# A transformer block with two mixtures of experts: a fixed order for TensorE in the first stage, counts made last, sixteen zero products, and three shared experts ahead of the tiles

## The chip, the cores and the metric

The kernel runs on one core of one Trainium2 chip. That core has five engines with a queue each: TensorE (PE, matrix products; its weight loads are shown apart as PEld), VectorE (DVE), ScalarE (ACT), GpSimd (POOL) and SyncE (SP, which here only issues DMAs). Sixteen DMA engines move the data. The metric is the time of one execution on the device in microseconds, lower is better. Before the change the median of 9 runs is 551.19 us (546.62 to 552.5).

## What is computed

The input x has 4 blocks of 512 rows with 256 columns. It goes through half a feed-forward layer, an attention and the same half layer again:

```python
x = x + 0.5 * ffn(layernorm(x))
x = x + attn(layernorm(x))     # 3 heads of width 256, mean over the heads, then fc_w, fc_b
x = x + 0.5 * ffn(layernorm(x))

def ffn(x):                    # 16 experts, the best 2 of each row
    scores = sigmoid(x @ gate_w)
    selected = top_k(scores + expert_bias, 2)
    top = scores[selected] / sum(scores[selected])
    shared = (silu(x @ shared_gate_w) * (x @ shared_up_w)) @ shared_down_w
    routed = sum(comb[:, e] * ((silu(g_e) * u_e) @ experts_down[e]) for e in range(16))
    return shared + routed     # g_e, u_e = split(x @ experts_gate_up[e])
```

Everything is float32. The attention's softmax runs over the axis of the queries, and the kernel works with A = Wq^T Wk / 16 and G = Wv^T fc_w^T / 3 for each head, which it makes once in the first stage.

## The kernel before

**Stages.** In the profiled execution the first stage lasts until 80 us: x and all weights are loaded, all four blocks b are normalised and routed, A and G are made, and two shared experts are computed. Then come 42 expert tiles of 128 rows each (80 to 151 us), a branch for more tiles that only an uneven routing needs, the other two shared experts, and the attention, block by block (168 to 434 us). From its second block on, the attention's loop also normalises and routes the block before for the second feed-forward layer. At the end come that layer's tiles and shared experts.

**Order.** The program is written for a scheduler that places each instruction in its engine's queue by priority, which follows the program text, and by an estimate of when its inputs are ready. Engines run their queues strictly in order; across engines there are semaphores. Three helpers bend the order without adding a wait on other engines: `after(ins, other)` (L184) puts one instruction behind another of its engine, `tc.issue_after(ins)` does so for all that a `with` block issues on the engine of `ins`, and `apart` (L189) declares that two accesses don't touch the same rows.

**One block in the first stage.** `moments(b)` (L196) makes mean and variance on DVE, the root on ACT and the reciprocal on DVE. `layernorm_T` (L215) normalises the rows to `xn` (on DVE for block 0, L233; on ACT for blocks 1 to 3, L228), transposes them on TensorE (L238), copies the two halves `xnT` out of PSUM (L242 on ACT, L244 on ACT or L246 on DVE) and doubles `xn` on ACT (L248), because each row is sent to two experts. `scores` (L282) multiplies with `gate_w` (L290, sixteen products of 16 columns a block), and `gate` (L298) takes the sigmoid. `router` (L308) picks the best two on DVE, counts on TensorE, with ten bfloat16 products against a matrix of ones or a triangle (L349 to L359), how many rows of the same expert stand ahead, and gets from that each row's place in a buffer sorted by expert. It also adds the block to the running count `seen`, makes the column totals `counts` with one more product (L374), and has POOL write the 512 rows twice to that buffer in DRAM, in 8 indirect DMAs (L393, "scatters").

**From the router to the tiles.** `ends` (L402) makes the end of each expert's rows from the last `counts`. `blanks` (L409, L417) writes 128 empty rows behind each expert's end, a DMA each on SP, whose place SP reads from `end` (L412). `early` (L465) computes on DVE a table of the first 9 tiles, which only blocks 0 to 2 can fill; `table` (L490) that of the rest. `load` (L503, L511) reads the place of a tile from the table into a register of SP and loads its rows as `xg`; `experts` (L549) runs a tile through transposes (L556), products (L572), sigmoid (L578), a second transpose (L587) and the down product (L594), and has POOL scatter the result (L599). SP's queue holds the first 8 blanks, the 9 first loads, the other 8 blanks, and then the rest.

**Shared expert.** `shared` (L522) makes `pg` and `pu` with four products of 512 columns each (L529) in two PSUM buffers, sigmoid on ACT (L534), two products on DVE (L535, L536), eight products `po` of 256 columns (L541), and adds them to x on DVE (L546). Its `pg` and `pu` share three PSUM buffers ("mm") with A and G (L713, copied out by ACT at L717).

**The first stage's text (L664 to L733).** Block 0: moments, scores; then moments 1, gate 0, router 0, scores 1, gate 1, moments 2 and 3, router 1, then for blocks 2 and 3 scores, gate, router, and last `ends` and `early`. A and G stand behind the ranks of router 0, shared experts 0 and 1 behind A and G and behind the early table, `table` behind those.

Of the kernel before, what the change touches and what calls it, by code (L numbers as in the profile page):

```python
# [17 lines left out]
P = 128  # L18
# [3 lines left out]
def tile_macaron_block(  # L22
# [62 lines left out]
    MAGIC = 12582912.0  # L85
    CEIL = 0.5 - 1.0 / (2 * P)
# [17 lines left out]

    xs = []
    for b in range(B):
        xb = acts.tile([P, NJ, H], F32, tag=f"x{b}", name=f"x{b}")
        nc.sync.dma_start(out=xb, in_=x[b].rearrange("(p j) h -> p j h", j=NJ))
        xs.append(xb)
# [73 lines left out]

    def after(ins, other):  # L184

        info = mybir.DependencyInfo(mybir.DependencyClass.NoSync, mybir.DependencyReason.DATA)
        tc.add_manual_dep(ins.ins, other.ins.name, info, reason="order")
# [6 lines left out]
    turned, rooted = {}, {}  # L194
# [20 lines left out]
    def layernorm_T(b, which, dispatch=False, moms=None):  # L215
# [10 lines left out]
        for j in range(NJ):  # L226
            if off is not None:
# [4 lines left out]
            else:  # L232
                nc.vector.tensor_scalar(  # L233
# [3 lines left out]
            for c in range(NC):  # L237
                nc.tensor.transpose(  # L238
                    pts[c][:, j * P : (j + 1) * P], xn[0][:, j, c * P : (c + 1) * P], ident
                )  # L240
        xnT = acts.tile([P, NC, N], F32, tag=f"xnT{b}", name=f"xnT_{n}")
        ins = nc.scalar.copy(xnT[:, 0, :], pts[0])  # L242
        if off is not None:
            ins = nc.scalar.copy(xnT[:, 1, :], pts[1])  # L244
        else:
            turned[n] = nc.vector.tensor_copy(xnT[:, 1, :], pts[1])  # L246
        if dispatch:
            after(nc.scalar.copy(xn[1][:, :, 0:H], xn[0][:, :, 0:H]), ins)  # L248
        return xnT, xn

    class Ffn:


        def __init__(self, which):
# [25 lines left out]
            self.xn, self.s, self.got = {}, {}, {}  # L280

        def scores(self, b, moms=None):  # L282
# [4 lines left out]
            for j in range(NJ):  # L287
                t = b * NJ + j
                for c in range(NC):
                    self.scored = nc.tensor.matmul(  # L290
# [5 lines left out]
                    )  # L296
# [12 lines left out]
        def router(self, b):  # L309
# [39 lines left out]
            nc.tensor.matmul(rank[:, 0:n], ones, over_t(region), start=True, stop=False)  # L349
            nc.tensor.matmul(rank[:, 0:n], ones, over_t(self.seen[:, b, :]), start=False, stop=False)  # L350
            for k in range(NK):
                for j in range(NJ - 1):
                    nc.tensor.matmul(
                        rank[:, (j + 1) * NE : n], ones,
                        ones_k[:, k, j : j + 1, :].to_broadcast([P, NJ - 1 - j, NE]),
                        start=False, stop=False,
                    )
            for k in range(NK):
                self.ranked = nc.tensor.matmul(  # L359
                    rank[:, 0:n], before, ones_k[:, k], start=False, stop=(k == NK - 1)  # L360
                )
# [12 lines left out]
            nc.tensor.matmul(  # L374
                self.counts[:, b * NE : (b + 1) * NE], ones, self.seen[:, b + 1, :],
                start=True, stop=True,
            )
# [23 lines left out]

        def ends(self):  # L402
# [6 lines left out]
        def blanks(self, e0=0, e1=NE):  # L409

            for e in range(e0, e1):
                r = nc.values_load(  # L412
                    self.end[0:1, e : e + 1], engines=(mybir.EngineType.SP,),
# [3 lines left out]
                ins = nc.sync.dma_start(  # L417
# [105 lines left out]
        def shared(self, b, cols=P):  # L523
# [3 lines left out]
            for ps, wt in ((pg, sg), (pu, su)):  # L527
                for c in range(NC):
                    nc.tensor.matmul(  # L529
                        ps, wt[:, c, :], self.xnT[b][:, c, :], start=(c == 0), stop=(c == NC - 1)  # L530
                    )
            h = work.tile([P, N], F32, tag="h", name=f"h_{n}")
            g = work.tile([P, N], F32, tag="g", name=f"g_{n}")
            nc.scalar.activation(g, pg, AF.Sigmoid)  # L534
            nc.vector.tensor_tensor(g, g, pg, ALU.mult)  # L535
            nc.vector.tensor_tensor(h, g, pu, ALU.mult)  # L536
            for j0 in range(0, NJ, 2):
                po = psum.tile([P, 2, H], F32, tag="dn", name=f"po_{n}_{j0}")
                for j in (j0, j0 + 1):
                    for p0 in range(0, P, cols):  # L540
                        self.shared_on_pe = nc.tensor.matmul(  # L541
                            po[p0 : p0 + cols, j - j0, :],
                            h[:, j * P + p0 : j * P + p0 + cols], sd, start=True, stop=True,
                        )
                xp = xs[b][:, j0 : j0 + 2, :]
                last = nc.vector.scalar_tensor_tensor(xp, po, 0.5, xp, ALU.mult, ALU.add)  # L546
            return last

# [120 lines left out]
    with tc.issue_after(turned["ln0_0"].ins):  # L669
# [3 lines left out]
    with tc.issue_after(m[1][3].ins):  # L673
        ffn.router(0)
    ranked = ffn.ranked
    ffn.scores(1, m[1])
    scored = [ffn.scored]
    ffn.gate(1)
    with tc.issue_after(ffn.last.ins), tc.issue_after(ffn.gated.ins):
        m.extend(moments(b, f"ln0_{b}", True) for b in (2, 3))  # L680
    with tc.issue_after(m[3][3].ins):
        ffn.router(1)
    for b in (2, 3):
        ffn.scores(b, m[b])
        ffn.gate(b)
        with tc.issue_after(ffn.last.ins):
            ffn.router(b)
    with tc.issue_after(ffn.last.ins):
        ffn.ends()
        ffn.early()  # L690


    with tc.issue_after(ranked.ins):
        fcT = weights.tile([P, NC, H], F32, tag="fcT", name="fcT")
        for c in range(NC):
            pt = psum.tile([P, H], F32, tag="dn", name=f"ptfc_{c}")
            for o in range(NC):
                nc.tensor.transpose(
                    pt[:, o * P : (o + 1) * P], fcw[:, o, c * P : (c + 1) * P], ident
                )  # L700
            nc.scalar.copy(fcT[:, c, :], pt)
        A, G = [], []
        for h in range(NH):
            wq, wk, wv = (wi[:, h] for wi in watts)
            for res, name, lhs, rhs, by in (
                (A, "A", wq, wk, float(H) ** -0.5),
                (G, "G", wv, fcT, 1.0 / NH),
            ):
                t = weights.tile([P, NC, H], F32, tag=f"{name}{h}", name=f"{name}{h}")
                pw = psum.tile([P, NC, H], F32, tag="mm", name=f"pw{name}{h}")  # L710
                for ec in range(NC):
                    for c in range(NC):
                        made = nc.tensor.matmul(  # L713
                            pw[:, ec, :], lhs[:, c, ec * P : (ec + 1) * P], rhs[:, c, :],
                            start=(c == 0), stop=(c == NC - 1),
                        )
                nc.scalar.mul(t, pw, by)  # L717
                res.append(t)


    done = ffn.last
    for b in (0, 1):
        with tc.issue_after(made.ins), tc.issue_after(done.ins):
            done = ffn.shared(b)
    with tc.issue_after(done.ins):
        ffn.table()
    ffn.blanks(0, NE // 2)
# [18 lines left out]
    for b in range(B // 2, B):  # L746
        ffn.shared(b)
    for b in range(B):
# [41 lines left out]
        if b > 0:  # L790
# [3 lines left out]
            if b == B - 1:  # L794
                ffn2.early()
# [29 lines left out]
    ffn2.router(B - 1)  # L825
# [78 lines left out]
```

## Time and profile before

| what | before |
|---|---|
| median of 9 runs | 551.19 us |
| the profiled execution | 553.12 us |
| its span | 551.3 us |
| TensorE busy, whole span | 502.8 us (91%) |
| weight loads, DVE, ACT, POOL busy | 355.9, 276.2, 191.5, 161.7 us |
| mean granted TensorE clock | 0.964 |

The span runs from the first to the last instruction of the program, the profiled execution's own time contains 1.8 us more around it. Busy times are sums over an engine's instructions; those of TensorE are modelled at their ends. The next lines are the page's slices: the span in 40 equal parts of 13.8 us, each digit the busy share in tenths, for TensorE, DVE, ACT, POOL and the mean DMA engine. The first six digits are the first stage.

```profile
PE   4789399999989999999999999999999967999984
DVE  4556155545745651158702676144482642455565
ACT  3471015666540620018200382004600323466630
POOL 2456504555530100001050011400032063356550
DMA  7993355557210100110021100100014044546755
```

In lists of the timeline a line gives the start and length in microseconds, the engine (SPq is SP's queue, which only issues), the line of the kernel, the operation, what is written from what, the shapes, how many instructions are merged, and in brackets how long the engine had been idle and what ended that ("issue" or "remote" where the profile names no one).

### The profile page before, as it was taken

The page shows a single profiled execution, that of the slowest core. Times are in us where ns is not written, and L with a number is a line of the kernel's source. Part 1 is how long each engine was busy: PE and PEld are TensorE (multiplying, and loading weights), DVE is VectorE, ACT ScalarE, POOL GpSimd, SP SyncE. Part 2 cuts the span into 40 slices and gives each one's busy share as a digit, 9 for nine tenths or more (in the row PEclk, how much of TensorE's full clock was granted, in tenths as well). Part 3 has the DMA queues.
Part 4 walks back from the last instruction along what each step waited for, and adds up shares of the span by engine and source line. Part 5 has one row for each costly group of instructions (what it writes and reads, how often), then busy time and mean ns, then how long its engine had stood idle before and what let it go on. Part 6 is the DMA issues. An engine that isn't in the chain of part 4 may idle for free. (4 is left out here: it accounts for less than half of the span.)

```text
span 551.3 us, 7562 instructions
## 1 busy us (share of the span) xinstructions
PE 502.8 (91%) x2120; PEld 355.9 (65%) x2120; DVE 276.2 (50%) x985; ACT 191.5 (35%) x446; POOL 161.7 (29%) x195
## 2 busy tenths in 40 slices
PE   4789399999989999999999999999999967999984
PEld 3577058888645478744886458854688644778842
DVE  4556155545745651158702676144482642455565
ACT  3471015666540620018200382004600323466630
POOL 2456504555530100001050011400032063356550
PEclk9998779999989999999999999999999896999989
DMA  7993355557210100110021100100014044546755
GB/s 265 356 366 132 125 147 162 164 165 238 102 46 0 39 0 1 38 38 2 0 78 38 38 2 10 68 0 0 1 38 117 9 145 154 153 146 182 261 182 191
DMA packets 38427, 57.89 MB, mean 105 GB/s; under 512 B 5360, under 2 KB 30192, under 8 KB 38384
## 3 DMA queue, kind: packets, MB, share of 16 engines
q1 hardware_dynamic: 30176, 37.49, 21.9%
q0 software_dynamic: 7104, 19.47, 9.8%
q10 hardware_dynamic: 1104, 0.42, 0.3%
q8 instruction: 19, 0.31, 0.2%
q14 instruction: 24, 0.20, 0.1%
HBM read 31.04 MB, written 26.31 MB: 104 GB/s over the span
## 5 line engine op out<-in xcount | busy, mean ns | idle before, releaser
L393 POOL DMA_INDIRECT xn_d<-xn_ln,pos x64 | 62.5, 976 | 154.5 <-DVE v L807 73.8
L599 POOL DMA_INDIRECT y_d<-ey,to x84 | 82.1, 977 | 72.4 <-ACT xt L560 47.6
L572 PE MATMUL peg<-gu,xt 128*128 x336 | 88.5, 387 | 1.9 <-issue 1.2
L773 PE MATMUL psc<-y,xnT_lna 128*128 128x512 f32 x192 | 84.5, 595 | 0.4 <-ACT ex L780 0.4
L815 PE MATMUL pa<-v,ex 128*128 128x256 f32 x384 | 83.5, 379 | 0.0
L815 PEld LDWEIGHTS pa<-v,ex 128*128 128x128 f32 x384 | 73.0, 190 | 9.9
L773 PEld LDWEIGHTS psc<-y,xnT_lna 128*128 128x128 f32 x192 | 36.0, 190 | 44.4 <-issue 42.2
L572 PEld LDWEIGHTS peg<-gu,xt 128*128 128x128 f32 x336 | 58.3, 193 | 9.4 <-issue 2.9
L780 ACT ACTIVATE ex<-psc,nmax 128x512 f32<-128x512 f32 x48 | 32.8, 686 | 85.4 <-DVE nmax L777 84.2
L589 DVE COPY hT<-pht 128x128 f32<-128x128 f32 x84 | 24.4, 290 | 65.1 <-issue 21.2
L594 PE MATMUL pey<-dn,hT 128*128 x168 | 51.8, 391 | 1.8 <-DVE hT L589 1.8
L598 ACT ACTIVATE ey<-pey,xg 128x256 f32<-128x256 f32 x84 | 39.6, 473 | 28.4 <-issue 16.9
L751 POOL TENSOR_TENSOR x<-x,fcb_bc 128x1024 f32<-128x1024 f32 x4 | 9.4, 2351 | 129.8 <-DVE xn_lna L233 129.8
L777 DVE TENSOR_REDUCE nmax<-psc 128x1 f32<-128x512 f32 x48 | 32.9, 686 | 26.1 <-PE psc L773 26.1
L803 PE MATMUL pv<-G,xnT_lna 128*128 128x256 f32 x192 | 44.6, 385 | 0.0
L758 PE MATMUL py<-xnT_lna,A 128*128 128x512 f32 x96 | 42.0, 592 | 0.0
L820 DVE TENSOR_TENSOR x<-x,pa 128x256 f32<-128x256 f32 x16 | 6.7, 421 | 68.9 <-PE pa L815 68.9
L803 PEld LDWEIGHTS pv<-G,xnT_lna 128*128 128x128 f32 x192 | 35.1, 190 | 4.3
L578 ACT ACTIVATE sig<-peg 128x128 f32<-128x128 f32 x84 | 23.3, 278 | 41.4 <-PE peg L572 20.2
L560 ACT COPY xt<-pxt 128x256 f32<-128x256 f32 x84 | 30.6, 366 | 12.0 <-PE pxt L556 10.2
L556 PE MATMUL pxt<-ident,xg 128*128 128x128 f32 x168 | 33.1, 281 | 0.0
L758 PEld LDWEIGHTS py<-xnT_lna,A 128*128 128x128 f32 x96 | 18.2, 190 | 21.3 <-issue 21.0
(164 smaller groups left out, 630.2 us busy)
## 6 DMA issues: line engine op xcount, KB each, us to landing
xg<-xn_d SPq DMA_DIRECT2D x84, 129.0 KB
xn_d<-nowhere SPq DMA_DIRECT2D x34, 129.0 KB
gu<-ffn_experts_gate_up_dram SPq DMA_DIRECT2D x4, 1024.0 KB
yg<-y_d SPq DMA_DIRECT2D x8, 512.0 KB
y<-y_d SPq DMA_DIRECT2D x6, 512.0 KB
x<-in_L_attn_x_dram SPq DMA_DIRECT2D x4, 512.0 KB
dn<-_L_ffn_experts_down_dram SPq DMA_DIRECT2D x2, 1024.0 KB
out_dram<-x SPq DMA_DIRECT2D x3, 512.0 KB
```

The costliest lines, as they stand in the source:

```text
L393: ins = nc.gpsimd.indirect_dma_start(out=self.xn_v[k * NT + b * NJ + j], out_offset=bass.IndirectOffsetOnAxis(ap=pos[:, k, j : j + 1], axi ...
L556: ins = nc.tensor.transpose(pt[:, c, :], xg[:, c * P : (c + 1) * P], ident)
L572: nc.tensor.matmul(pg, xt[:, c, :], gu[:, bass.ds(e, 1), c, :], start=(c == 0), stop=(c == NC - 1),)
L594: self.downed = nc.tensor.matmul(py, hT, dn[:, bass.ds(e, 1), :], start=True, stop=True)
L598: nc.scalar.mul(y, py, xg[:, H + 1 : W])
L599: ins = nc.gpsimd.indirect_dma_start(out=self.y_v[i], out_offset=bass.IndirectOffsetOnAxis(ap=tos[i], axis=0), in_=y, in_offset=None,)
L758: nc.tensor.matmul(py, A[h][:, c, fc * P : (fc + 1) * P], xnT[:, c, :], start=(c == 0), stop=(c == NC - 1),)
L773: nc.tensor.matmul(pscore, xnT[:, c, m * P : (m + 1) * P], ys[h][:, c, :], start=(c == 0), stop=(c == NC - 1),)
L777: nc.vector.tensor_reduce(nmax[:, m : m + 1], pscore, AX.X, ALU.max, negate=True)
L780: nc.scalar.activation(ex[:, m, :], pscore, AF.Exp, bias=nmax[:, m : m + 1], accum_out=z[:, m : m + 1],)
L803: nc.tensor.matmul(pv, xnT[:, c, m * P : (m + 1) * P], G[h][:, c, :], start=(c == 0), stop=(c == NC - 1),)
L815: nc.tensor.matmul(pa, es[h][:, m, j * P : (j + 1) * P], vs[h][:, m, :], start=(h == 0 and m == 0), stop=(h == NH - 1 and m == NJ - 1),)
```

## The change

- **Loads.** x of block 0 is loaded in two halves of two row groups each.
- **Zero products.** At the very start DVE clears a tile of 128 x 512 bfloat16, and TensorE multiplies it sixteen times (`WARM = 16`) into a PSUM buffer that nobody reads.
- **A fixed order on TensorE.** Each group of TensorE's instructions in the first stage gets a name (`mark`), and `in_turn` puts every instruction of a group behind the last of the group before, over 39 named groups: T is a transpose of a block, S its scores, K and L the ranks for the first and second choice, A, fcT and G the attention's weights, U and D the two halves of a shared expert, C the counts.
- **The text's order.** Router 1 now comes directly behind router 0, and the moments of blocks 2 and 3 behind router 1. A and G come ahead of scores 2 and 3. The up half of shared expert 0 stands between scores 3 and router 2, its DVE products between router 2 and router 3. Counts of all four blocks come behind router 3 (in the second layer, three of them ahead of its early table and the last behind its last router). Behind `ends` come shared expert 1, the early table, shared expert 2, the second table.
- **Shared experts.** Three instead of two ahead of the tiles, so only number 3 is left between the tiles and the attention.
- **Smaller moves.** Block 1 is normalised on DVE instead of ACT, the second half of block 0's transposed rows is copied by ACT instead of DVE, the doubling copies of blocks 0 and 1 and the copy of block 1's transposed rows stand behind a sigmoid on ACT. The ranks of the first choice are all issued ahead of those of the second. `blanks` gets parameters for another queue, which no call uses.

```diff
+    idle = const.tile([P, 512], BF16, tag="idle", name="idle")
+    nc.vector.memset(idle, 0.0)
+    nothing = psum.tile([P, 512], F32, tag="mm", name="nothing")
+    for _ in range(WARM):
+        nc.tensor.matmul(nothing, idle[:, 0:P], idle, start=True, stop=True)
...
+        for j in range(0, NJ, 2 if b == 0 else NJ):
+            js = slice(j, j + (2 if b == 0 else NJ))
+            nc.sync.dma_start(out=xb[:, js], in_=rows[:, js])
...
+    def mark(name, ins):
+        groups.setdefault(name, []).append(ins)
+        return ins
+    def in_turn(*names):
+        for one, two in zip(names, names[1:]):
+            for ins in groups[two]:
+                after(ins, groups[one][-1])
...
-            if off is not None:
+            if off is not None and n != "ln0_1":
                 nc.scalar.activation(xn[0][:, j, 0:H], ...
...
-        if off is not None:
+        if off is not None or n == "ln0_0":
             ins = nc.scalar.copy(xnT[:, 1, :], pts[1])
...
             for k in range(NK):
                 for j in range(NJ - 1):
-                    nc.tensor.matmul(
-                        rank[:, (j + 1) * NE : n], ones,
+                    count(
+                        "KL"[k], rank[:, (j + 1) * NE : n], ones,
                         ones_k[:, k, j : j + 1, :].to_broadcast([P, NJ - 1 - j, NE]),
-            for k in range(NK):
-                self.ranked = nc.tensor.matmul(
-                    rank[:, 0:n], before, ones_k[:, k], start=False, stop=(k == NK - 1)
-                )
+                count("KL"[k], rank[:, 0:n], before, ones_k[:, k], stop=(k == NK - 1))
...
-            nc.tensor.matmul(
-                self.counts[:, b * NE : (b + 1) * NE], ones, self.seen[:, b + 1, :],
-                start=True, stop=True,
-            )
...
+        def count(self, b0, b1):
+            for b in range(b0, b1):
+                mark(f"C{self.w}_{b}", nc.tensor.matmul(
+                    self.counts[:, b * NE : (b + 1) * NE], ones, self.seen[:, b + 1, :],
+                    start=True, stop=True,
+                ))
```

The first stage's text after the change, with the loops that make A and G left out:

```diff
     ffn.scores(0, m[0])
-    with tc.issue_after(turned["ln0_0"].ins):
+    with tc.issue_after(normed["ln0_0"].ins), tc.issue_after(copied["ln0_0"].ins):
         m.append(moments(1, "ln0_1", True))
     with tc.issue_after(rooted["ln0_1"].ins):
         ffn.gate(0)
+    ffn.scores(1, m[1])
+    after(copied["ln0_1"], ffn.gated)
+    after(doubled["ln0_0"], ffn.gated)
+    with tc.issue_after(normed["ln0_1"].ins):
         ffn.router(0)
     ffn.gate(1)
+    after(doubled["ln0_1"], ffn.gated)
+    with tc.issue_after(ffn.last.ins):
+        ffn.router(1)
     with tc.issue_after(ffn.last.ins), tc.issue_after(ffn.gated.ins):
         m.extend(moments(b, f"ln0_{b}", True) for b in (2, 3))
...
+    for b in (2, 3):
+        ffn.scores(b, m[b])
+        with tc.issue_after(rooted["ln0_3"].ins):
+            ffn.gate(b)
+    ffn.shared_up(0)
+    with tc.issue_after(m[3][3].ins):
+        ffn.router(2)
+    with tc.issue_after(ffn.last.ins):
+        ffn.shared_down(0)
+    with tc.issue_after(ffn.gated_up.ins):
+        ffn.router(3)
+    ffn.count(0, B)
+    with tc.issue_after(ffn.last.ins):
+        ffn.ends()
+    with tc.issue_after(ffn.last.ins):
+        ffn.shared(1)
+    with tc.issue_after(ffn.gated_up.ins):
+        ffn.early()
+    with tc.issue_after(ffn.last.ins):
+        done = ffn.shared(2)
     with tc.issue_after(done.ins):
         ffn.table()
+    in_turn(
+        "Tln0_0", "S0_0", "Tln0_1", "S0_1", "K0_0", "L0_0", "A00", "A01", "A10", "K0_1", "A11",
+        "L0_1", "A20", "A21", "fcT", "G00", "G01", "G10", "G11", "G20", "G21",
+        "Tln0_2", "S0_2", "Tln0_3", "S0_3", "K0_2", "L0_2", "U0_0", "K0_3", "L0_3", "C0_0",
+        "C0_1", "C0_2", "C0_3", "D0_0", "U0_1", "D0_1", "U0_2", "D0_2",
+    )
     ffn.blanks(0, NE // 2)
...
-    for b in range(B // 2, B):
-        ffn.shared(b)
+    ffn.shared(3)
...
             if b == B - 1:
+                ffn2.count(0, B - 1)
                 ffn2.early()
...
     ffn2.router(B - 1)
+    ffn2.count(B - 1, B)
```

## The prediction

> **What bounds the kernel now.** I first read the busy time by stage (stretch and its length, busy us of PE, weight loads, DVE, ACT and POOL, granted clock, DMA share, GB/s).
>
> ```profile
> 0.00:80.00 80.00, 55.00 (x226) 40.47 (x227) 36.95 (x171) 26.18 (x46) 35.13 (x64) 0.89 0.72 235
> 80.00:151.40 71.40, 69.84 (x380) 57.30 (x378) 42.71 (x206) 43.22 (x125) 38.95 (x42) 1.00 0.53 164
> 151.40:168.00 16.60, 14.93 (x46) 8.62 (x47) 7.64 (x14) 6.81 (x10) 4.39 (x4) 0.90 0.12 43
> 168.00:434.00 266.00, 265.06 (x1009) 176.87 (x1007) 128.20 (x347) 69.40 (x136) 31.70 (x35) 1.00 0.08 27
> ```
>
> TensorE idles 25 us in the first 80 and hardly at all from there to 434. A microsecond off the first stage is one off the end, and TensorE work taken from the later stages into those idle 25 us is gained too. Then the timeline of the first stage on POOL (start, length, what, idle before and its releaser): the first scatter of row blocks 0, 1 and 2, and the last of all.
>
> ```profile
> 19.30 1.15 POOL L393 DMA_INDIRECT xn_d<-xn_ln,pos  x1 [15.34 <-DVE st_ln L201]
> 33.20 0.98 POOL L393 DMA_INDIRECT xn_d<-xn_ln,pos  x1 [3.52 <-DVE xn_ln L388]
> 45.38 0.99 POOL L393 DMA_INDIRECT xn_d<-xn_ln,pos  x1 [2.06 <-ACT fcT L701]
> 64.50 0.97 POOL L393 DMA_INDIRECT xn_d<-xn_ln,pos  x1 [0.30 <-issue]
> ```
>
> Neighbours start 1.27 us apart, so 32 scatters need 40.8 us; they took 46.2, with two waits for a router of 3.5 and 2.1 us. Last, the timeline between the blanks' first issue and the first expert tile.
>
> ```profile
> 51.38 8.90 SPq L417 DMA_DIRECT2D xn_d<-nowhere  x4
> 60.33 0.20 DVE L461 TENSOR_REDUCE fe<-fp 128x1 f32<-128x48 f32 x1 [1.27 <-DVE fo L457]
> 61.73 0.60 ACT L717 ACTIVATE A<-pwA 128x512 f32<-128x512 f32 x1 [10.58 <-issue]
> 68.19 0.60 ACT L717 ACTIVATE G<-pwG 128x512 f32<-128x512 f32 x1 [5.86 <-remote]
> 70.06 7.55 SPq L511 DMA_DIRECT2D xg<-xn_d  x9
> 79.86 0.60 PE L556 MATMUL pxt<-ident,xg 128*128 128x128 f32 x4
> ```
>
> From about 52.7 to 68.3, while SP's blanks and POOL's scatters run together, nearly every wait is late: a blank takes 2.2 us (0.83 after 78), a dependent DVE step 1.4 us, and ACT takes up a product that ended at 52.2 only at 61.7. I call this **the slow stretch**. The second layer shows it again, from 446 to 457.6, where blanks and scatters overlap too (DVE waits 9.2 us there). It ends 2.8 us after the last scatter's issue ends (65.47). TensorE then does three quarters of two shared experts in 11.5 us, from 68.3 to the tiles at 79.86, at a granted clock of 0.5 until 74.8.
>
> **The change part by part.**
>
> *Halved load of x0.* At the 354 GB/s of 10 to 20 us, 256 KB is 0.7 us: block 0's moments end 0 to 0.7 us earlier. I take 0.5.
>
> *Sixteen zero products.* No bf16 product of 512 columns is in the trace. Below: bf16 products of 64 columns start 0.029 us apart at 17.0, which is 0.23 for 512 and 3.7 us for all. Above: f32 products of 512 columns start 0.855 apart at half clock, 13.7 us. From about 1.1 us they end at 4.8 or 14.8. The first transpose can't start before 7.25 now and the last ends at 9.0, so the low end costs nothing and the high end makes everything 7 us late. I take 0.43 each, between the two (that is also the f32 spacing at full clock): done at 8.0, cost nothing.
>
> *What they buy.* The same sixteen score products of a block, in two stretches (busy PE, weight loads, DVE, ACT, then clock, DMA, GB/s):
>
> ```profile
> 9.60:13.30 3.70, 3.59 (x16) 3.48 (x16) 0.00 (x0) 0.02 (x1) 1.00 1.06 370
> 40.60:42.60 2.00, 1.97 (x17) 1.87 (x16) 0.00 (x0) 0.00 (x0) 1.00 0.97 295
> ```
>
> The first runs at half speed though the clock column says 1.00 (the first record of the clock is at 40.7). Full speed would save 0 to 1.65 us a block. I take 0.8 for block 0: the clock that was granted at 40.7 was back at 0.5 at 44.1, after little work.
>
> The Trainium skill, "TensorE: Matmul & The Clock Gate" (Part 1), has the clock rise after one window of about 3.4 us of sustained work; by it blocks 0 and 1 save 1.65 us each. The same page, in its table of what matters for kernels, lets an idle gap of about 3 us take it back, and in Part 4 doesn't count transposes as work, which speaks against this edit: the gain would be 0.
>
> *DVE and ACT of block 0 and 1.* ACT copies both halves (second done at 10.1, not 9.9), DVE is free 1.9 us sooner for block 1's moments, and normalises block 1 itself (1.39 us, where ACT took 2.06). Sigmoid 0 comes at 12.0 to 13.4 (now 13.28). But the rank products K0, L0 now stand behind S1 on TensorE: sigmoid 0.2, ACT's doubling copy 1.05 and two copies 1.1, then S1 1.94 to 3.6 put its end at 16.3 to 19.3, ranks 0.5, three DVE steps 0.9. pos is ready at 17.7 to 20.7 (now 18.08), the first scatter at 18.9 to 21.9 (now 19.30). I take 20.0: a loss of 0.7.
>
> *Router 1 before moments 2 and 3.* It ended at 32.40 because both moments (3.3 us) and a square-root table came first. It takes 4.9 us, so it ends near 25, before block 0's scatters do (30.2). The idle 3.5 us goes. Late next: router 2, behind moments, normalising on ACT (2.06), twelve G products, T2, S2, T3, S3 on TensorE. I have it at 41 to 43 (now 44.7) against POOL free at 40.4: the 2.1 us idle stays.
>
> *Router 3 behind shared expert 0.* U0 (3.4 to 6.8 us) and DVE's h0 stand before it: it ends at 49 to 53.5 (now 50.6). Scatters end at 62 to 64, I take 63.0: 2.5 us earlier. Blanks start at 52, 0.6 later. The slow stretch then ends at 65.9.
>
> *Early table behind shared expert 1.* In the slow stretch ACT's sigmoid 1 waits as ACT's A and G did, so h1 comes at 67.5 and the 4.3 us that such a table takes undisturbed (442.5 to 446.8) puts the first load at 71.8, against 70.06 now. Its cover was SP, busy with blanks until 69.5 while the table was done at 61.9; that cover is gone. If h1 gets through inside the stretch, loads start at 68.
>
> *TensorE up to the tiles.* All left after the stretch: from h1 at 67.5 D1 3.4, U2 5.1 (half of it at half clock), 0.75 for h2, D2 1.9: 78.7. With D1 and part of U2 done inside: 72. I take 75.5, so **4.4 us** off 79.86.
>
> *Shared expert 2 out of the stretch 154.5 to 167.4.* Eight products at 0.428 and eight at 0.214: 5.14 us. Today 2 and 3 hide each other's wait for h; alone, 3 holds two of three PSUM buffers from 159.4 to 161.2 and the attention's products can fill half of that: 0 to 2 back, I take 1.0. Gain **4.1 us**.
>
> *Counts last, second layer.* Three bf16 products of 0.17 us, ahead of a table that has TensorE idle around it; the last count is ready before DVE's end at 442.4 asks for it. Nothing; without that cover 0.5.
>
> **Sum.** 553.12 (span 551.3 and 1.8 around it) − 4.4 − 4.1 = 544.6. That execution lay 1.9 above the median of 551.19, so 542.7: **543**, and 538 to 547 from the bounds of 72 and 78.7 for the tiles.
>
> **Rivals.** *The slow stretch shrinks.* For: it needs scatters and blanks together, and if router 3 and U1 are early, h1, the table and D2 are through with it. Tiles then start near 67: 12.9 + 4.1 off, 534. Against: blanks still follow router 3 and ten scatters still follow them.
>
> *The work comes back.* TensorE is asked for one more expert before the tiles; if that chain binds, the tiles start 4.1 us later, at 84, and the moved expert is worth nothing: 551. For: U2, h2 and D2 are strictly one after the other. Against: 25 us idle.
>
> *The fixed order holds the routers up.* T2 and S2 stand behind all of G, which waits for two ACT copies of fcT; ACT takes A, fcT, the root and the normalising in one queue. If the root is behind G's last eviction (about 33), xn2 is at 37, S2 at 42, S3 at 46, router 2 at 49, U0 at half clock to 56, router 3 at 61, scatters to 71, the slow stretch to 74, tiles at 89: +9.1 − 4.1, 556. It decides from router 2 ending after 46 or so. For: today the same products fill gaps freely. Against: ACT is idle two thirds of the stage.
>
> That the zero products change nothing in the clock is held in the bounds above (0.8 us).
>
> **How the numbers follow.** Forecast 0.46, shrunken stretch 0.20, work comes back 0.14, order holds up 0.20. A measurement tells about 0.5% (2.8 us) from no change: faster 0.66, same 0.14, slower 0.20. The range takes in most of both outer cases: 532 to 556; the likeliest alone is 538 to 547.
>
> **What would show it.** First scatter at 19 to 22 and no idle before block 1's; last scatter issue ending at 62 to 64; blanks of over 2 us until some 2.8 us after that; first load at 68 to 72; first tile's transposes at 72 to 79; one shared expert, not two, after the tiles; block 0's score products under 3.5 us if the clock is up. Wrong if the slow stretch doesn't come back, or if router 2 or 3 ends past 46 or 55.

## The result, and the profile after

The changed kernel takes 563.37 us (median of 20 runs, 557.54 to 568.42), the kernel before 551.50 in the same comparison (62 runs): a ratio of 1.0208, 95% interval 1.0185 to 1.0232. It is 2.1% slower, 20 us above the forecast and 7 above its range. The profiled spans are 563.3 and 551.3 us.

Every ratio below is to the kernel before of the same job, for that kernel took 551.5 us here and 549.6 in the job of e11 to e14, but 529.4 to 530.3 in the other jobs.

The stages of the changed kernel (stretch, its length, then busy us of PE, weight loads, DVE, ACT and POOL, granted clock, DMA share, GB/s):

```profile
0.00:95.00 95.00, 66.53 (x259) 46.15 (x260) 40.26 (x179) 25.28 (x44) 34.99 (x64) 0.73 0.56 188
95.00:166.00 71.00, 67.54 (x361) 55.73 (x360) 38.01 (x185) 40.04 (x119) 36.15 (x39) 0.98 0.56 170
166.00:180.00 14.00, 11.43 (x41) 6.03 (x40) 8.54 (x31) 9.41 (x15) 7.20 (x6) 1.00 0.28 97
```

The first stage is 95 us long where it was 80, and TensorE idles 28 us of it instead of 25, though a shared expert more was put into it. The timeline shows what grew. First, block 1 to block 2 (start, length, engine, line, what, idle before it and its releaser):

```profile
21.43 1.15 POOL L414 DMA_INDIRECT xn_d<-xn_ln,pos  x1 [17.47 <-DVE eq L365]
...
31.74 0.49 ACT L228 ACTIVATE std_ln<-mv_ln,eps 128x4 f32<-128x4 f32 x2
...
42.13 0.60 ACT L736 ACTIVATE G<-pwG 128x512 f32<-128x512 f32 x1 [9.90 <-issue]
42.62 1.08 ACT L252 ACTIVATE xn_ln<-x,off_ln,rstd_ln 128x256 f32<-128x256 f32 x2
...
59.01 0.17 DVE L393 CAST pos<-r 128x8 int32<-128x8 f32 x1
59.96 0.98 POOL L414 DMA_INDIRECT xn_d<-xn_ln,pos  x1 [17.84 <-issue]
```

Sixteen scatters now run without a pause from 21.43 to 41.68. ACT takes the square roots at 31.74 and then nothing for 9.90 us, though the product that it copies out next, the first G, had ended near 32.4. It goes on when the scatters are through. It wasn't waiting for its own instructions to be fetched: between 24.4 and 62.5 us no queue that carries instructions moved a packet. Block 2's normalising stands behind that eviction in ACT's queue, so router 2 ends at 59.2 (about 44.3 before) and POOL idles for 17.84 us. Then the end of the stage:

```profile
70.23 14.04 SPq L446 DMA_DIRECT2D xn_d<-nowhere  x8
...
82.45 0.60 ACT L562 ACTIVATE g<-pg 128x512 f32<-128x512 f32 x1 [19.99 <-remote]
...
90.47 0.15 DVE L486 TENSOR_SCALAR fo<-fr 128x1 int32<-128x1 f32 x1
...
91.38 7.56 SPq L540 DMA_DIRECT2D xg<-xn_d  x9
...
94.97 0.60 PE L594 MATMUL pxt<-ident,xg 128*128 128x128 f32 x4
...
112.14 0.44 PE L594 MATMUL pxt<-ident,xg 128*128 128x128 f32 x2 [2.69 <-DMA xg<-xn_d]
```

A second late stretch holds the sigmoid of shared expert 1, whose input was ready near 74, until 82.45. The early table follows h1 and ends at 90.6, the loads follow the table, the tiles start at 94.97 instead of 79.86. Tile ten then waits another 2.69 us for its rows: SP issues its load behind eight blanks, and these behind nine loads that started only 3.6 us ahead of the first tile (9.8 before). The sum, from one landmark to the next, in both profiles:

| Stretch | before | after | difference |
|---|---|---|---|
| up to the first tile's transposes | 79.86 | 94.97 | +15.1 |
| the tiles | 72.14 | 76.94 | +4.8 |
| behind the tiles, up to attention's first scores | 24.78 | 18.02 | −6.8 |
| the rest | 374.5 | 373.4 | −1.2 |

That makes the 12.0 us between the spans. The tiles' +4.8 holds tile ten's 2.69 us and a stretch at half clock right behind it (113.2 to 116.6). The −6.8 is the shared expert that no longer stands behind the tiles (5.1 us of products) and 3.4 us at half clock (153.1 to 156.5) that only the profile before has there.

### The profile page after: what moved, and what is told of

The parts are those of the page before. It is cut to its first block, busy times and chain, and to the rows that moved or that the text cites. A ratio compares the mean times of both kernels' runs of the same rounds, so it can differ in the third digit from the quotient of the medians.

```text
span 563.3 us, 7592 instructions
## 1 busy us (share of the span) xinstructions
PE 508.0 (90%) x2136; PEld 357.5 (63%) x2136; DVE 276.2 (49%) x989; ACT 189.8 (34%) x443; POOL 161.5 (29%) x195
## 5 line engine op out<-in xcount | busy, mean ns | idle before, releaser
L627 DVE COPY hT<-pht 128x128 f32<-128x128 f32 x84 | 24.4, 290 | 69.0 <-issue 22.7
L873 DVE TENSOR_TENSOR x<-x,pa 128x256 f32<-128x256 f32 x16 | 6.7, 421 | 69.5 <-PE pa L868 65.5
```

## The experiments

**The same two kernels in another job** (no edit).

> The changed kernel once more, as it stands, because another chip gave the kernel before 530 us where it had been 551. If the slow stretch is a property of the kernel: the same loss to the kernel before (1.02), block 1's scatters unbroken, ACT taking up the first G about 10 us late, block 2's first scatter near 60. If it depends on the chip: no such stretch, block 2's first scatter at 45 to 48, a ratio between 0.99 and 1.01.

> The kernel before once more, for its profile on this chip. If the slow stretch is a property of the kernel: first tile's transposes near 80 and ACT's late eviction of A at 52 to 62 as before. If it depends on the chip: first tile's transposes at 68 to 73, no wait of ACT over 3 us between 45 and 70.

The changed kernel: 533.79 against 529.99, ratio 1.0087 (1.0050 to 1.0125). Timeline of the kernel before in this job: end of router 2, of router 3, blanks, table, loads, first tile.

```profile
40.83 0.17 DVE L368 CAST pos<-r 128x8 int32<-128x8 f32 x1 [0.17 <-DVE den L383]
...
47.84 0.30 DVE L368 CAST pos<-r 128x8 int32<-128x8 f32 x1 [0.17 <-DVE den L383]
...
49.36 6.84 SPq L417 DMA_DIRECT2D xn_d<-nowhere  x8
...
51.55 0.15 DVE L457 TENSOR_SCALAR fo<-fr 128x1 int32<-128x1 f32 x1
...
57.23 8.64 SPq L511 DMA_DIRECT2D xg<-xn_d  x9
...
62.99 0.60 PE L556 MATMUL pxt<-ident,xg 128*128 128x128 f32 x4
```

And of the changed kernel in it:

```profile
45.16 0.17 DVE L393 CAST pos<-r 128x8 int32<-128x8 f32 x1
...
49.36 0.69 DVE L570 TENSOR_TENSOR h<-g,pu 128x512 f32<-128x512 f32 x1 [0.40 <-PE pu L558]
...
54.59 0.17 DVE L393 CAST pos<-r 128x8 int32<-128x8 f32 x1 [0.17 <-DVE den L404]
...
55.91 6.79 SPq L446 DMA_DIRECT2D xn_d<-nowhere  x8
...
67.01 7.55 SPq L540 DMA_DIRECT2D xg<-xn_d  x9
...
69.89 0.64 PE L594 MATMUL pxt<-ident,xg 128*128 128x128 f32 x4
...
88.03 0.69 PE L594 MATMUL pxt<-ident,xg 128*128 128x128 f32 x2 [3.51 <-DMA xg<-xn_d]
```

Here no wait of the first stage is late: eight blanks take 6.8 us beside the scatters, where they took 17.9 in the kernel before and 14.0 in the changed one. Without the late stretch the kernel before starts its tiles 16.9 us earlier, at 62.99. So the loss has two parts. One is in the order itself: tiles 6.9 us later (69.89 against 62.99) and a wait of 3.51 at tile ten (0.54 in the kernel before), less the expert that moved. The other, 8.2 of the 15.1 us, comes only where waits are late. These two profiles lie 9.7 us apart (spans of 534.6 and 524.9), the medians 3.8: single profiles show where time goes, the medians how much.

**The fixed order taken out, and three theories of the late waits** (one execution each, in a job without late waits).

```diff
e1  -    in_turn("Tln0_0", "S0_0", ..., "U0_2", "D0_2")
e2  loads of gu, dn: moved behind  ffn = Ffn(0)
e2  +            if which:
e2  +                after(self.fill, ffn.first[-1]); after(fill_y, ffn.first[-1])
e3  +    pause = nc.gpsimd.tensor_copy(late_off, m[3][2])
e3  +    for ins in ffn.scatters[1]: after(ins, pause)
e4  weigh("G", ...): moved behind ffn.count(0, B); "G00" ... "G21" behind "D0_0"
```

> TensorE's instructions are no longer held to a fixed place; everything else is as in the changed kernel. If the fixed order is what costs (block 2's transposes and scores stand behind all products G): the first scatter of block 2 comes back from 59.96 to about 46 to 48, the first tile's transposes from 94.97 to about 82, the time from 563 to about 550. If the waits themselves are late (ACT takes up G only when block 1's scatters have been issued, at 42.1, and the normalising of block 2 stands behind it on ACT, whatever TensorE's order is): the first scatter of block 2 stays at 55 to 60 and the time at 558 to 564.

> SP's fills of xn_d and y_d go ahead of the loads of the experts' weights (first layer) and behind the first tile loads (second layer), so that none of them runs beside block 0's and 1's scatters at 38 to 42. Theory of the DRAM writes (a slow stretch needs SP's writes beside POOL's scatters): ACT takes up the first G by 36 instead of 42.1, block 2's first scatter goes by 53, the time is about 555. Theory of the long run (16 scatters without a pause beside any other transfer are enough) and theory of the fixed order: no difference, G at 41 to 43, 561 to 565.

> POOL waits for the end of block 3's moments (a copy of their result, about 31.8) between the scatters of block 0 and of block 1, as it did by chance before the change; nothing else differs. Theory of the long run: ACT takes up the first G at 32 to 34 in the pause instead of at 42.1, block 2's normalising ends near 36, its first scatter goes at 46 to 50 instead of 59.96, the time is 550 to 556 although block 1's scatters end a microsecond later. Theories of the DRAM writes and of the fixed order: the pause gives nothing back, the first scatter of block 2 stays at 58 to 61, the time at 562 to 566.

> The products G, with their evictions by ACT, are moved behind router 3 and shared expert 0, so that block 2's and 3's normalising, transposes and scores stand behind A and fcT only. Theory of the fixed order: block 2 is normalised from 32.5, its scores end by 40, its first scatter goes at 43 to 46, the first tile's transposes come at about 82, the time is 550 or less. Theory of late waits (each hand-over between ACT and TensorE is late while scatters run, whatever is handed over): block 2's scores still end only when block 1's scatters have been issued, at 43 to 47, its first scatter goes at 50 to 55, the time is 554 to 560.

Times, with the kernel before at 530.29: e1 530.99, e2 535.07, e3 533.75, e4 541.70. In this job nothing was late to begin with, so e2 and e3 say nothing on the late waits; e3's pause was 0.16 us, as the moments were done by then. The free order (e1) puts the first tile at 69.05 instead of 69.89 and is 2.8 us under the changed kernel's median of the other job, within its spread of 530.73 to 536.95: nothing shows that the fixed order is the loss, and one execution can't tell 2.8 us. Moving G behind the routers (e4) seems to cost: its twelve products then stand ahead of U1, and the tiles start at 76.03.

**The zero products, and the third shared expert.**

```diff
e5  -    for _ in range(WARM):
e5  -        nc.tensor.matmul(nothing, ...)
e5  +    nc.tensor.matmul(nothing, ...)
e6  -    with tc.issue_after(ffn.last.ins):
e6  -        done = ffn.shared(2)
e6  -    ffn.shared(3)
e6  +    for b in (2, 3): ffn.shared(b)
```

> One zero product instead of sixteen. By the forecast (they lift the clock for block 0's scores and cost nothing): block 0's scores take 0.4 to 1.7 us longer, the time is 0 to 1.5 us longer. By the rival (the clock they lift is lost again by 11 us, so that nothing is bought): the time is within 1 us of the changed kernel. If they stand in the way: 0.5 to 2 us shorter.

> Shared expert 2 goes back behind the tiles, beside expert 3, as before the change. By the forecast (expert 2 lies in idle time ahead of the tiles): tiles start 0 to 1 us earlier and the time is 3 to 4 us longer than the changed kernel's. By the rival of the work that comes back: tiles start 4 us earlier and the time is the same within 1 us.

e5: 534.97, ratio 1.0084 (1.0037 to 1.0131), no difference to sixteen that can be told; the intervals are some 2 us wide to either side. The products do what they are for: block 0's scores take 2.22 us with them and 3.66 without (3.15 in the first profile). In e5's profile the first scatter comes at 22.58 instead of 19.92, of which a later load of x0 is 0.9, and the first tile at 73.59 instead of 69.89; the span is 1.3 us longer. What the products are worth at the end stays open. e6: 540.15, ratio 1.0184 (1.0149 to 1.0218). Against 1.0087 that is 0.97%, or 5.1 us (give or take 2.7), for the moved expert. The profiles say the same: from the first transpose behind the tiles to attention's first scores e6 takes 23.24 us and the changed kernel 18.09, each with 3.4 us at half clock. In e6 TensorE waits 5.45 us for the first tile's rows: the loads hold the tiles, so the third expert ahead of them doesn't hold them up.

**VectorE's order, the ranks, the places.**

```diff
e7  router(3); count; ends; shared_down(0); early; shared(1); shared(2)
    # instead of: shared_down(0); router(3); count; ends; shared(1); early; shared(2)
e8  "Tln0_3", "K0_2", "L0_2", "S0_3"      # instead of "Tln0_3", "S0_3", "K0_2", "L0_2"
e9  "S0_2", "U0_0", "Tln0_3", "K0_2", "L0_2", "S0_3", "D0_0", "U0_1", "K0_3", "L0_3", ...
e9  +    after(ffn.opened, copied["ln0_3"])
e10 (kernel before)  for b in (0, 1, 2): ... done = ffn.shared(b);  behind the tiles: ffn.shared(3)
```

> VectorE's order of before on the changed kernel: router 3, the ends and the early table come ahead of shared expert 0's products h; TensorE's fixed order stays. Numbers are for a chip like the one of the changed kernel's second profile (534.6 us, tiles at 70.2). Theory of the serial chain (router 3 behind h0, the early table behind h1): router 3 ends at 50 to 51 instead of 55.0, blanks start at 52 instead of 56.2, the table is done by 58 instead of 66.5, the first tile's transposes come at 66 to 68, the ratio to before is 1.000 to 1.005. Theory that only TensorE's order costs: table earlier, but the tiles still at 69 to 72 because U1, U2 and D2 follow D0 on TensorE, ratio 1.006 to 1.012.

> In the fixed order block 2's rank products K2, L2 go ahead of block 3's score products S3 instead of behind them; nothing else. Theory: in the changed kernel router 2 waits on TensorE for S3 (its second half takes 8.2 us where router 1's took 4.9), so router 2 ends at 42 to 43 instead of 45.6, block 2's first scatter goes at 43 to 43.5 instead of 46.1, the last scatter's issue ends 2.5 to 3 us earlier, near 63.5; S3 and U0 come later by the rank products' 0.5 to 1 us, so tiles stay at 70 to 71 and the time within 1.5 us of the changed kernel's. Rival: the scatters' end is what the rest waits for, and the time falls by 2.5 us with them.

> The fixed order with other places: U0 into TensorE's idle time ahead of T3, K2 and L2 ahead of S3, D0 and U1 ahead of router 3's K3 and L3, and sigmoid 0 behind block 3's copies on ACT; VectorE's order and everything else as in the changed kernel. Theory of the serial chain: h0 is done by 44, U1 by 50, h1 by 53, the early table by 58, tiles at 60 to 63, and with shared expert 2 out of the later stage the time is 6 to 9 us under before (ratio 0.983 to 0.990). If each of the pieces moved only changes places with another wait: tiles at 66 to 70, ratio 0.997 to 1.008.

> The kernel before with shared expert 2 moved ahead of the tiles, as the only part of the change. By the forecast's term (the moved expert lies in idle time and gives 4.1 back): tiles at most 2 us later, ratio 0.993 to 0.997. By the rival of the work that comes back (U2, h2 and D2 one after the other ahead of the tiles): tiles 4 to 5 us later, ratio 0.999 to 1.002.

e7: 526.62, ratio 0.9940 (0.9908 to 0.9973). Router 3 before h0 and the table before h1 turn the loss into a small gain, where 1.000 to 1.005 was expected: 1.5% between c_after and e7, with TensorE's order, the zero products and everything else left as they are. Its timeline:

```profile
50.43 0.17 DVE L393 CAST pos<-r 128x8 int32<-128x8 f32 x1
...
56.26 0.14 DVE L486 TENSOR_SCALAR fo<-fr 128x1 int32<-128x1 f32 x1
...
60.02 8.14 SPq L540 DMA_DIRECT2D xg<-xn_d  x9
```

Router 3 ends 4.2 us earlier than in c_after, the table 10 us, the loads 7. The first tile comes at 66.44, 3.5 earlier, and tile ten doesn't wait any more: 6.4 lead of the loads instead of 2.9.

e8: 534.65, ratio 1.0101 (1.0048 to 1.0153). Router 2 ends at 40.8 instead of 45.3, block 2's scatters go at 41.88, and nothing is gained: POOL waits 3.98 us for router 3, which still stands behind h0, and the last scatter is issued at 64.68 instead of 65.23, 0.55 earlier where 2.5 to 3 was expected.

e9: 528.86, ratio 0.9970 (0.9925 to 1.0015), no difference to before that can be told, where a gain of 6 to 9 us was expected. U0 ahead of T3 takes 5.4 us, at a granted clock of 0.72 from 36 to 42, and T3 ends 2.5 us later, and TensorE waits 3.04 us until 66.51 for the rows of the first load, issued at 61.80 while scatters run.

e10: 527.57, ratio 0.9981 (0.9950 to 1.0011). In the kernel before the tiles move from 62.99 to 68.13, 5.1 later, and the 5.1 us saved behind them come back. The expert is free only behind loads that are late anyway.

**One move alone, a combination, and no write of SP beside a scatter** (a job with late waits: kernel before 549.6).

```diff
e11 "S0_2", "g0_0", "Tln0_3", "u0_0", "K0_2", "L0_2", "S0_3", "D0_0", "g0_1", "K0_3", "L0_3", ...,
    "u0_1", "g0_2", "D0_1", "u0_2", "D0_2"     # gate and up products apart; table ahead of h1
e12 ends; early; shared(1); shared(2)          # router 3 still behind h0
e13 router(3); ends; shared_down(0); shared(1); early; shared(2)
e14 fills as in e2;  own = copy of end by POOL behind the last scatter, read by SP for its blanks
```

> Fixed order with shared expert 0's gate product in TensorE's gap ahead of T3 and its up product behind T3, K2 and L2 ahead of S3, D0 and expert 1's gate product ahead of K3, expert 1's up product and expert 2's gate product right behind the counts; on VectorE the early table ahead of h1, and expert 0's additions behind h1. Theory of the serial chain: router 2 ends at 43 to 44, ends at 51, the table at 56, h1 at 57, D2 at 62 to 64, tiles at 62 to 65, ratio to before 0.985 to 0.992. If the tiles are held by their loads instead (a tile's rows land late while scatters run): tiles at 66 to 68, ratio 0.993 to 0.998.

> The early table goes back ahead of shared expert 1 on VectorE; router 3 stays behind shared expert 0's h. Theory that the table's move is the larger cost: table done at 60 instead of 66.5, loads from 63 instead of 67.3, tiles at 66 to 68, ratio 0.995 to 1.002. Theory that it is router 3's move (everything behind it 4 to 5 us late): tiles still at 69 to 71, as U1, h1, U2, h2, D2 follow D0 as before, ratio 1.005 to 1.011.

> Router 3 and the ends go back ahead of shared expert 0's h on VectorE; the early table stays behind shared expert 1's h. Theory that router 3's move is the larger cost: router 3 ends at 50 to 51, h1 by 59, the table by 64, tiles at 66 to 68, ratio 0.993 to 1.000. Theory that it is the table's: tiles at 69 to 71, ratio 1.003 to 1.010.

> The changed kernel with none of SP's DRAM writes beside a scatter: fills ahead of the experts' weights (first layer) and behind the first loads (second), the first eight blanks behind the last scatter's issue. On a chip with late waits (kernel before near 551): by the theory of the DRAM writes the hand-overs come in time, block 2's first scatter near 47, blanks at 68 to 76, tiles near 79 instead of 95, ratio near 1.005; by that of the long run block 2's first scatter stays near 60 and the tiles at 90 or later, ratio 1.02 or more. On a chip without (before near 530): blanks and loads only move back, tiles at 75 to 78, ratio 1.014 to 1.022, and the theory stays open.

Ratios: e11 1.0148 (1.0110 to 1.0186), e12 1.0203 (1.0160 to 1.0245), e13 1.0243 (1.0193 to 1.0292), e14 1.0186 (1.0132 to 1.0240); first tiles at 84.43, 93.35, 92.15 and 90.86. Late waits cover whatever e12 and e13 do: which of the two moves costs more stays open. e11 is the best of the four, but still loses. The useful one is e14. Its timeline around both stretches:

```profile
32.20 0.60 ACT L743 ACTIVATE G<-pwG 128x512 f32<-128x512 f32 x1 [3.58 <-PE pwG L739]
...
41.38 0.60 ACT L743 ACTIVATE G<-pwG 128x512 f32<-128x512 f32 x1 [7.60 <-issue]
...
75.95 0.60 ACT L560 ACTIVATE g<-pg 128x512 f32<-128x512 f32 x1 [16.71 <-issue]
...
78.25 4.05 SPq L444 DMA_DIRECT2D xn_d<-nowhere  x5
```

SP writes nothing between 33 and 78, and ACT is late at 41.38 and at 75.95 all the same (the input of the second was ready near 70.4). So the writes of SP aren't what makes waits late. In e11 the scatters of blocks 2 and 3 start at 58.11 and VectorE's steps keep their pace until 64.6; from 65.2 each dependent one waits 1.1 us:

```profile
66.61 0.16 DVE L485 SCALAR_TENSOR_TENSOR fr<-row,fr 128x1 f32<-128x1 f32 x1 [1.12 <-DVE fv L473]
...
68.02 0.15 DVE L486 TENSOR_SCALAR fo<-fr 128x1 int32<-128x1 f32 x1 [1.07 <-DVE fp L487]
...
80.72 0.69 DVE L580 SCALAR_TENSOR_TENSOR x<-po,x 128x512 f32<-128x512 f32 x1 [5.62 <-remote]
```

That is the sixth or seventh scatter of an unbroken run, and the last late wait ends 2.5 us after the run does (78.2). The other late stretches begin between about the sixth and the eleventh scatter of a run: before at 52.7 (run from 45.38), after at some 28 to 32 (run from 21.43) and 71 (run from 59.96), e14 at some 29 to 33 (run from 19.3).

A run of eight can do it too. The kernel before pauses for 3.5 us ahead of the run from 33.20, and yet near that run's end, first in the first profile and then in the job without late waits:

```profile
43.23 0.29 DVE L364 TENSOR_TENSOR rk<-one,psk 128x128 f32<-128x128 bf16 x1 [4.08 <-PE psr L290]
44.84 0.22 ACT L303 ACTIVATE s<-psr 128x64 f32<-128x64 f32 x1 [4.41 <-remote]
...
39.91 0.29 DVE L364 TENSOR_TENSOR rk<-one,psk 128x128 f32<-128x128 bf16 x1 [0.84 <-PE psk L359]
42.99 0.22 ACT L303 ACTIVATE s<-psr 128x64 f32<-128x64 f32 x1 [2.76 <-PE psr L290]
```

The rank product that VectorE takes up at 43.23 had ended at 39.96, and the scores that ACT takes at 44.84 had ended at 42.59. The run of eight from 19.30 shows nothing late.

**Pauses in the run of scatters.**

```diff
e15, e16 +                if w == 0:
e15, e16 +                    self.landed = nc.gpsimd.tensor_copy(xn[k][:, :, H], place[:, k, ts])
e15, e16 +  (before each scatter)  after(ins, self.landed)
```

> The changed kernel, in whose first layer POOL waits after every fourth scatter until these four have landed (an estimate from the loads' 2 to 4 us from issue to landing: 2 us each, the last scatter's issue 4 to 16 us later than without). If the kernel before is near 550 (late waits): by the theory of the long run the hand-overs come in time, ACT takes up all G by 35, block 2's first scatter goes near 47 instead of 57 to 60, tiles at 70 to 75 instead of 94, ratio 1.005 to 1.013 instead of 1.021. If something else makes them late: G again at 41 to 43, tiles at 90 or later, ratio 1.018 or more. If the kernel before is near 530 (no late waits): the pauses only cost, ratio 1.008 to 1.016.

> The order of e11 with the same pauses. If the kernel before is near 550: by the theory of the long run tiles at 63 to 68 and a ratio of 0.970 to 0.985, since the kernel before keeps its own late stretch; if something else makes the waits late, tiles at 84 or later and a ratio near 1.015. If the kernel before is near 530: tiles at 62 to 67, ratio 0.985 to 0.998.

This job had no late waits (kernel before 529.4), so the theory that a long run makes waits late wasn't tried by them. The pauses cost: e15 541.22, ratio 1.0236 (1.0154 to 1.0318), e16 537.55, ratio 1.0166 (1.0069 to 1.0264). POOL waits 5.34 and 5.71 us for four scatters to land while the weights are loaded and 1.4 to 3.5 later, not 2; the loads of the first tiles then wait for block 2's last scatter, at 72.44 and 72.09 (67.01 in c_after).

## Why the prediction was wrong

**The term that failed: TensorE up to the tiles.** The sum has it at −4.4 (tiles at 75.5); it measured +15.1 (94.97). The other term, 4.1 for the moved expert, held. Two steps under the failed term were wrong.

**The first: the slow stretch.** The forecast took it for a thing of SP's blanks beside POOL's scatters, at one place, with an end 2.8 us behind the last scatter. The changed kernel shows one already at 32 to 42, before any blank (the first is at 70.23; SP's fills stand beside it, from 31.09 to 36.9): the late copy of G at 42.13 put router 2 at 59.2, and with it the last scatters, the second late stretch (to 82.45) and the tiles. e14 shows both with no write of SP between 33 and 78. What the traces agree on is that late waits lie in the later part of a run of scatters and just behind it. The forecast saw POOL's pause of 3.5 us ahead of block 1 vanish (right: 21.43 to 41.68 unbroken) and put it down as time saved. That joining two runs of eight into one of sixteen brought the stretch to the place where block 2 is normalised fits what was seen, but isn't shown: the kernel before has late waits near the end of a run of eight, behind a pause. The 2.1 us of idle that the forecast kept ahead of block 2 were themselves such a wait (0.16 at 43.39 in the second job). Whether a pause inside a run keeps late waits away wasn't tried where waits are late, and their cause stays open.

**The second: what the stretch hid.** The serial part (router 3 behind h0, the table behind h1, h2 behind the table) was added up, but set against tiles at 79.86, a start that the stretch had made late in the kernel before. "Its cover was SP, busy with blanks until 69.5" was true of that profile alone (they ended at 69.27); with punctual waits the blanks end at 56.2 in the kernel before, and at 62.7 in the changed one, where the table, done at 66.6, then holds the loads (67.01). The order itself costs 6.9 us of tile start and 3.5 at tile ten; undoing VectorE's two moves (e7) brings back 3.5 of the 6.9 and the wait at tile ten.

**Router 2.** Forecast 41 to 43, measured 59.2, and 45.3 where nothing is late. Two causes: normalising behind the late eviction of G on ACT (not the root, as the rival had it: the roots came at 31.74), and K2, L2 behind S3 in the fixed order, which the list of names shows and the sum left out: 4.5 us by e8. "Wrong if ... router 2 or 3 ends past 46 or 55" held on both (59.2 and 69.1). The rival *the fixed order holds the routers up* had the sign and the deciding point, and 556 of the 563; its mechanism was half right, as e1, which frees TensorE's order, moves the first tile by less than 1 us. That the rival came within 8 us of the measured time is in part luck: for router 2 it held the root and G's products responsible, and no late wait.

**The other terms.** The moved expert was sized 4.1 and is worth 5.1 to 5.3 by the profiles (e6 against the changed kernel, and 21.71 us before against 16.37 after up to attention's first scores, both at full clock, in the second job): the 1.0 for a wait of expert 3 alone didn't come. In the kernel before it is worth nothing that can be told (e10, 0.2% give or take 0.3), as *the work comes back* says. The zero products were done at 6.2 in the first profile (forecast 8.0) and 7.3 in the second job, before the first transpose, so they held nothing up, as taken; their gain at block 0's scores was 0.4 to 1.4 us, around the 0.8 taken, and what of it reaches the end stays open (e5). Halving the load of x0 was sized 0.5 earlier and came out 0.6 later in the first profile: the second half's statistics waited for DMA until 5.76, the mean was there at 6.73 instead of 6.10. In the second job it made no difference (5.98 against 6.01). The first scatter came at 21.43, inside the bound of 21.9, not at 20.0 (19.92 in the second job). Router 1 ended at 26.8, not 25. Nothing shows a cost of the late counts.

The granted clock of the changed kernel, by stretch (columns as above):

```profile
4.50:11.00 6.50, 4.18 (x24) 2.45 (x23) 4.61 (x20) 1.96 (x5) 0.00 (x0) 0.99 0.88 329
11.20:24.50 13.30, 12.84 (x59) 11.18 (x60) 8.90 (x41) 4.78 (x8) 2.46 (x3) 0.50 1.10 350
```

The clock was granted in full from 4.00 to 10.82, from 2.8 us behind the first zero product (1.24), and half of it after that; in the second job from 6.14 to 12.96, 4.9 us behind it. (The forecast's 40.7, 44.1 and 74.8 for the clock are 40.46, 43.87 and 74.59 in the trace.) The Trainium skill ("TensorE: Matmul & The Clock Gate", Part 1) has full speed after one free-running window of about 3.4 us; by an estimate from that page the 6.8 us of full speed are two such windows. Its table of what matters lets a gap of about 3 us take the clock back. Here the clock went with no gap longer than 1.7 us (6.21 to 7.87). If transposes don't count as work, which the forecast held possible, the gap is 3.5 us (6.21 to 9.75) and fits; but in the second job the clock went only 1.7 us behind the last score product (11.22), so the traces don't bear out the gap as the only cause.

## What to carry to other kernels

A cover read from one profile is only as good as the wait that makes it: before calling a step hidden, ask whether the hiding work is itself late for a reason that can go, and add up the chain as if it were punctual. When shared work is moved into idle time of one engine, put the steps that release other queues (the last router, the table that the loads need) ahead of it in every engine's order; here that alone was worth 1.5%. And before a wait is taken for a property of a kernel, profile that kernel in a second job: the late waits that this forecast was built on were gone there, and 21 us with them.

## What was not expected of the hardware

The same kernel took 530 us in four jobs, and 550 in the first measurement and one other job; the whole difference that the traces show lies in late hand-overs while scatters run (16.9 us at the first tile; and in the second layer one wait of VectorE of 9.15 us, before 457.6, where the 525 us profile has none over 3.2). What makes a job one or the other stays open; it isn't the chip's number alone, as chip 7 gave 530 in one job and 549.6 in another. The recording is a rival that no run here rules out: every run on record comes with a granted clock, so each was recorded, and the six profiles with late waits hold about 4,600 to 4,700 semaphore events, the fourteen without about 7,500, of the same programs. Their pages lack the landing times of DMAs that the others give (2.2 us for a tile's rows in the second job's profile of the kernel before, none in the first). The recording may suffer from the same thing or be part of the delay, and releasers such as "issue" and "remote" in those profiles are the less certain for it. In such stretches waits are late between TensorE and ScalarE (9.90 us), and even from one VectorE step to the next (1.1 us). The Trainium skill ("SBUF — State Buffer", "Who interferes with whom") knows a lock between GpSimd and VectorE, and says that TensorE and ScalarE never wait on others' ports; the 9.90 us are between just these two, so that rule doesn't explain them.

Four scatters of 128 rows take 5.3 to 5.8 us from the last one's issue to landing while the weights are loaded, and 1.4 to 3.5 us after that (e15, e16); the 2 us that the expectation estimated from the loads was far off for them.
